# A two-layer graph kernel on one core: the softmax sums of layer 1 made on VectorE with two small matmuls, in place of matmuls with ones over all columns

## The chip, the cores and the metric

The kernel runs on one core of a Trainium2 chip. The metric is the device time of one launch in microseconds, as the median of several runs. The time before is 2396.18 us, the median of 3 runs (2393.23 to 2396.19).

## The reference

64 graphs of 256 nodes with 512 features, and a 0/1 adjacency matrix for each. Two layers, all in float32:

```python
# layer 0 (one head)
fp     = x @ fc_w.T + fc_b                                   # [256, 512]
logits = (fp @ q_w.T + q_b) + (fp @ k_w.T + k_b).T           # [256, 256]
masked = leaky_relu(logits + (1 - adj) * -1e9, 0.01)
x1     = softmax(masked) @ fp + x
# layer 1 (8 heads of 64)
Q, K, V = x1 @ W_q + b_q, x1 @ W_k + b_k, x1 @ W_v + b_v
a, c    = x1 @ w_g[:512], x1 @ w_g[512:]
scores  = Q @ K.T / 8 + a[:, None] + c[None, :] + b_g + log(adj + 1e-9)
out     = softmax(scores) @ V + x1
```

A term that is the same for a whole row of scores falls out of a softmax. So in layer 1 the weight of node i for node j is exp(Q_i K_j / 8 + c_j) * (adj + 1e-9), divided by its sum over j. That sum, one for each of 8 heads and 256 nodes of a graph, is what the change is about.

## The kernel before

Two graphs make a group (`GP = 2`, 512 tokens), and there are 32 groups (`NG`). The products of 512 by 512 are done in a form with seven half-size products (`Product`, whose pieces are `p1` to `p7`, with `keep_*` read out by ScalarE and `sum_*` added by VectorE). Their matmuls all have line L399, their names are `pf` (layer 0's feature product, on the mixed features), `pq`, `pk` and `pv`.

The order of the work is written out by hand: in `step` and `attention_and_layer_0`, strings of piece names are issued one after the other, and each engine runs its instructions in that order. One step holds pieces of four groups: the end of layer 1 of `d` (D), the attention of `a` (A), layer 0 and the projections of `f` (F), and the loads and layer 0's logits of `n` (X). A step with all four begins, in this order, with:

- `pv.sum_11` (VectorE, L427), `scores:0` (TensorE L786, with two exponentials on ScalarE, L800), `sums` (layer 0's sums by products with ones, TensorE L583, read out by ScalarE, L588), `scores:1`, `pv.p3`, `pv.p4`;
- `mix:0` to `mix:3` (TensorE L614, then ScalarE L620), with `ysum` (VectorE L339), `recip` (L592, L593), and D's `divide:1` (VectorE L891), `complete:1` (L899) and `store:1` (DMAs on SP, L929);
- the product `pf`, whose results `pf.sum_*` (VectorE L485) are turned and sent through DRAM and back (`send`, VectorE L717 and SP L721; `fetch`, SP L732) to be there with features on the partitions (`x1T`);
- among these, A's `scores:2`, `attend:0` (TensorE L826, ScalarE L833), `sums_1:0`, `scores:3`, and later `attend:1`, `sums_1:1`;
- then `xsum` (VectorE L364), `pq.*` and `pk.*`, with `keys` (VectorE L500), A's `complete:0 store:0`, A's `turn:1` (VectorE L871) and `ratios_t:1` (L903), the dots of the next group (`dot_q`, `dot_k`, L500), its mask (`adjt`, L536), `residual` (ScalarE L757) and `turn_residual` (VectorE L771), `pv.*` and `weights` (VectorE L570, L574, ScalarE L575).

The attention keeps its weights as e[j, head, i] with j on the partitions, in two halves `jc`. `factor:u:jc` (VectorE L806) multiplies by the adjacency, and `both:u` (L813) adds the two halves, into `esum[u]`: 128 partitions by four heads by 256 nodes, with u = 0, 1 for the first graph and u = 2, 3 for the second. The sum over j is then over the 128 partitions:

- `sums_1:gr` (TensorE L842) does it with eight matmuls whose stationary operand is 32 columns, one of ones and the others zero, and whose moving operand is 256 columns of `esum`; four stand side by side in the array. The result is one bank, copied by ScalarE to `sms1` (L849).
- `ratios_t:gr` (VectorE L903) turns it by blocks of 32 by 32, and `ratios_r:gr` takes the reciprocal (L876) and spreads it over the partitions as `divide` needs it (L879, and four copies of 32 partitions, L882).
- `divide:gr` (L891) multiplies the turned output `osb` by it; `complete:gr` (L899) adds the residual.

PSUM has four single banks that go round (`bank`) and two pairs for the scores (`pair`). `pk.p2` takes the bank that `pq.sum_00` (VectorE L427) has read last. The reciprocals of several groups are kept (`recip1`, `NR` groups) and are compared with a range from time to time (`check`, `in_range`, L938 to L945). The last group has an order of its own at the end of `step` (`n is None`).

Of the kernel before, what the change touches and what calls it, by code (L numbers as in the profile page):

```python
# [25 lines left out]
def kernel(  # L26
# [17 lines left out]
    b_g: bass.AP,  # L44
    out: bass.AP,
):

# [41 lines left out]
    nc = tc.nc  # L89
# [63 lines left out]
    wq_row = const.tile([P, D], F32, tag="wq_row", name="wq_row")  # L153
    kqc = const.tile([P, 1], F32, tag="kqc", name="kqc")

    NR = 8
    recip0 = const.tile([P, NG, T], F32, tag="recip0", name="recip0")
    recip1 = const.tile([P, NR, GP, 2, N // B], F32, tag="recip1", name="recip1")

    def fast():  # L160
        main = ExitStack()
        with main:
# [45 lines left out]
            nc.gpsimd.memset(ones, 0.0)  # L208
            for n in range(2):
                nc.gpsimd.memset(ones[:, n, n : n + 1], 1.0)  # L210

            fc_nat = one.tile([P, T, D], F32, tag="xT", name="fc_nat")
            for c in range(NC):
# [70 lines left out]
            def constants_of_projections():  # L284


                pc = bank("pc")[:, 0:HALF]
                for c in range(NC):
                    for n, (w, o) in enumerate(((wq_sb, 0), (wq_sb, 1), (wv_sb, 0), (wv_sb, 1))):
                        nc.tensor.matmul(  # L290
                            pc[ts(n, RS), :], lhsT=fcb_col[:, c : c + 1].to_broadcast([P, RS]),
                            rhs=w[:, c, o * HALF : (o + 1) * HALF],
                            start=(c == 0), stop=(c == NC - 1), tile_position=(0, n * RS),
                            skip_group_check=True,
                        )
                rows = one.tile([P, HALF], F32, tag="st", name="pc_rows")
                nc.scalar.copy(rows, pc)

                def add():
                    pt = bank("pct")  # L300
                    for m in range(2):
                        nc.tensor.transpose(pt[:, ts(m, P)], rows[:, ts(m, P)], ident)
                    cols = pt[:, 0 : 2 * P].rearrange("p (m n r) -> p n m r", m=2, r=RS)
                    for n, col in enumerate((bq_col, bq_col, bv_col, bv_col)):
                        half = col[:, ts(n % 2, 2)]
                        nc.vector.tensor_tensor(half, half, cols[:, n, :, 0], ALU.add)
                    nc.vector.tensor_tensor(bv_col, bv_col, fcb_col, ALU.add)

                return add
# [195 lines left out]
            class Group:  # L505
# [70 lines left out]

                def sums(self):

                    sm = bank(f"sm0_{self.g}")[:, 0:P]
                    for jc in range(TPG):  # L580
                        for t in range(T):
                            gr, ic = divmod(t, TPG)
                            nc.tensor.matmul(  # L583
                                sm[ts(t, RS), :], lhsT=ones[:, 0, :], rhs=self.e0[:, jc, gr, ts(ic, P)],
                                start=(jc == 0), stop=(jc == TPG - 1), tile_position=(0, t * RS),
                            )
                    self.sms = one.tile([P, P], F32, tag="sms", name=f"sms_{self.g}")
                    nc.scalar.copy(self.sms, sm)  # L588
# [226 lines left out]
                def attend(self, gr):  # L815
# [3 lines left out]
                    for hg in range(2):  # L819
# [12 lines left out]
                                    )  # L832
                        nc.scalar.copy(self.oTs[gr][:, hg, :], po)  # L833

                def sums_1(self, gr):

                    g = self.g

                    sm = bank(f"sm_{g}_{gr}")[:, 0:N]
                    for hg in range(2):  # L840
                        for n in range(4):
                            nc.tensor.matmul(  # L842
                                sm[ts(n, RS), :], lhsT=ones[:, hg, :],
                                rhs=self.esum[2 * gr + hg][:, n // 2, n % 2, :],
                                start=(hg == 0), stop=(hg == 1), tile_position=(0, n * RS),
                                skip_group_check=True,
                            )
                    self.sms1[gr] = one.tile([P, N], F32, tag="sms1", name=f"sms1_{g}_{gr}")
                    nc.scalar.copy(self.sms1[gr], sm)  # L849

                def sums_of_e(self, gr):

                    g = self.g
                    sm = bank(f"sm_{g}_{gr}")[:, 0:N]
                    for hg in range(2):
                        for jc in range(TPG):
                            for n in range(4):
                                nc.tensor.matmul(
                                    sm[ts(n, RS), :], lhsT=ones[:, hg, :],
                                    rhs=self.e[2 * gr + hg, jc][:, n // 2, n % 2, :],  # L860
                                    start=(hg == 0 and jc == 0), stop=(hg == 1 and jc == TPG - 1),
                                    tile_position=(0, n * RS), skip_group_check=True,
                                )
                    self.sms1[gr] = one.tile([P, N], F32, tag="sms1", name=f"sms1_{g}_{gr}")
                    nc.scalar.copy(self.sms1[gr], sm)

                def turn(self, gr):
# [4 lines left out]

                def ratios_r(self, gr):
                    g, nb = self.g, N // B
                    rc = recip1[:, g % NR, gr]
                    nc.vector.reciprocal(rc, self.st.rearrange("p (b c) -> p c b", c=B)[:, 0:2, :])  # L876

                    rs = two.tile([P, 2, 2, nb], F32, tag="rs", name=f"rs_{g}_{gr}")
# [6 lines left out]
                    self.rs = rs  # L885

                def divide(self, gr):

# [1 line left out]
                    blocks = self.osb.rearrange("p (m c) -> p m c", c=B)  # L890
                    nc.vector.tensor_tensor(  # L891
                        blocks, blocks,
                        rs.rearrange("p a n b -> p (a n b)").unsqueeze(2).to_broadcast(
                            [P, NC * nb, B]
                        ), ALU.mult,
                    )
# [2 lines left out]
                    nc.vector.tensor_tensor(self.osb, self.osb, self.xb[gr], ALU.add)  # L899

                def ratios_t(self, gr):
                    self.st = one.tile([P, N], F32, tag="st", name=f"st_{self.g}_{gr}")
                    nc.vector.transpose(self.st, self.sms1[gr])  # L903

                def finish(self, gr):
# [4 lines left out]
                    for hg in range(2):  # L910
# [2 lines left out]
                        nc.vector.transpose(o, self.oTs[gr][:, hg, :])  # L913
                        nc.vector.tensor_tensor(  # L914
                            blocks, blocks,
                            self.rs[:, hg].rearrange("p n b -> p (n b)").unsqueeze(2).to_broadcast(
                                [P, 2 * nb, B]
                            ), ALU.mult,
                        )
# [10 lines left out]

            def in_range(lo, hi, name):

                n0, n1 = (hi - lo) * T, (hi - lo) * T * NH
# [14 lines left out]
            def attention_and_layer_0(D, A, F, X, check):  # L948

                A("pv.sum_11 scores:0")  # L950
                F("sums")
                A("scores:1 pv.p3 pv.p4 factor:0:0 factor:0:1 both:0 factor:1:0 pv.sum_10")
                A("factor:1:1 both:1")
                D("ratios_r:1")
                check()
                F("mix:0 mix:1 ysum:0 recip")
                D("divide:1")
                A("residual:1")
                F("mix:2 mix:3 ysum:1 ysum:2 ysum:3")
                D("complete:1 store:1")  # L960
                F("pf.p1 pf.keep_1 pf.p2 pf.p6 pf.sum_00 begin send:0:0 fetch:0:0")
                A("turn_residual:1")
                F("pf.p7 pf.p5")
                A("scores:2 attend:0 sums_1:0 scores:3 factor:2:0 factor:2:1")
                F("pf.sum_11 send:1:1 fetch:1:1")
                A("both:2 turn:0 ratios_t:0 factor:3:0")
                F("pf.p3 pf.sum_01 send:0:1 fetch:0:1")
                A("factor:3:1 both:3")
                F("pq.p1 pq.keep_1 pf.p4 pf.sum_10 send:1:0 fetch:1:0")
                A("attend:1 sums_1:1 ratios_r:0 divide:0")  # L970
                F("pk.p1 pk.keep_1")

            def check_ranges():
# [9 lines left out]

                return flag_ready

            checked = {}

            def step(d, a, f, n, check):

# [20 lines left out]
                    F("pq.p1 pq.keep_1 pk.p1 pk.keep_1")  # L1010
                F("xsum:0 xsum:1 xsum:2 pq.p6 keys:2 keys:3 keys:0 keys:1")
                X("load_x")
                A("complete:0 store:0")
                F("pq.p7 xsum:3")
                A("turn:1 ratios_t:1")
                F("pq.p2 pq.sum_00 pq.p5 pk.p2 pq.sum_11 copy:0 pq.p3 copy:1 copy:2 pk.sum_00 pq.p4")
                X("dot_q:0")
                F("pq.sum_10")
                X("dot_q:1 dot_q:2 dot_q:3 spread adjt")
                F("pk.p6 pk.p7 pk.p5 residual:0")  # L1020
# [2 lines left out]
                X("dot_k:2 dot_k:3")  # L1023
                F("turn_residual:0 pv.p1 pv.keep_1 pk.p3 pk.p4 pk.sum_10")
                if n is None:
                    A("ratios_r:1 divide:1 complete:1 store:1")
                    F("residual:1 turn_residual:1")

                    F("pv.p2 scores:0 pv.p6 pv.sum_00 factor:0:0 factor:0:1 scores:1 both:0 pv.p7")
# [8 lines left out]
                X("weights:0")  # L1038
                F("pv.sum_00 pv.p7 pv.p5")
                X("weights:1")  # L1040

            with tc.manual_schedule(engines=ENGINES):
                f = Group(0)
# [234 lines left out]
```

## Time and profile before

| | |
|---|---|
| median of 3 runs | 2396.18 us |
| the profiled execution | 2395.4 us, its span 2393.6 us |
| granted clock of TensorE | 0.998 |
| PE, busy | 2376.3 us, 99% |
| DVE (VectorE), busy | 1841.4 us, 77% |
| ACT (ScalarE), busy | 1002.9 us, 42% |
| `sums_1`: L842 on PE, 1008 records | 67.5 us |
| `ratios_t`: L903 on DVE, 64 | 25.8 us |
| `ratios_r`: L876, L879, L882 on DVE | 14.7, 11.6, 42.6 us |
| one step in the middle (1181.45 to 1254.90) | 73.45 us; PE busy 73.45, DVE 57.02, ACT 31.13 |

PE is TensorE's matmuls, PEld its weight loads. A float32 matmul of the program has two records in the profile, each with a weight load of its own. Where matmuls lie side by side in the array, the busy time counts their union once. A line of the timeline gives start, duration, engine, source line, operation, the tile written and the tiles read, the shape and the number of instructions merged; a number in brackets at its end is idle time before it, with what ended it.

### The profile page before, as it was taken

The page shows a single profiled execution, that of the slowest core. Times are in us where ns is not written, and L with a number is a line of the kernel's source. Part 1 is how long each engine was busy: PE and PEld are TensorE (multiplying, and loading weights), DVE is VectorE, ACT ScalarE, POOL GpSimd, SP SyncE. Part 2 cuts the span into 40 slices and gives each one's busy share as a digit, 9 for nine tenths or more (in the row PEclk, how much of TensorE's full clock was granted, in tenths as well). Part 3 has the DMA queues.
Part 4 walks back from the last instruction along what each step waited for, and adds up shares of the span by engine and source line. Part 5 has one row for each costly group of instructions (what it writes and reads, how often), then busy time and mean ns, then how long its engine had stood idle before and what let it go on. Part 6 is the DMA issues. An engine that isn't in the chain of part 4 may idle for free.

```text
span 2393.6 us, 36233 instructions
## 1 busy us (share of the span) xinstructions
PE 2376.3 (99%) x13947; PEld 1917.8 (80%) x13947; DVE 1841.4 (77%) x3126; ACT 1002.9 (42%) x1772; POOL 143.5 (6%) x103
## 2 busy tenths in 40 slices
PE   9999999999999999999999999999999999999997
PEld 5888787888878888888887888787888877887886
DVE  6778777777777778777878777777778877787776
ACT  3444344444344343444434443444444444443443
POOL 0000000000000000000000000000000000000000
PEclk9999999999999999999999999999999999999999
DMA  4122322323322333223232232332233322223212
GB/s 128 45 62 67 84 71 58 62 62 84 78 65 57 62 76 84 71 54 62 67 84 71 58 64 61 84 81 68 52 66 71 84 71 54 62 66 85 71 49 37
DMA packets 517274, 164.00 MB, mean 69 GB/s; under 512 B 415188, under 2 KB 478696, under 8 KB 517096
## 3 DMA queue, kind: packets, MB, share of 16 engines
q1 hardware_dynamic: 514440, 160.32, 29.6%
q8 instruction: 112, 1.84, 0.3%
q10 hardware_dynamic: 2656, 1.31, 0.2%
q14 instruction: 66, 0.54, 0.1%
HBM read 95.43 MB, written 66.12 MB: 67 GB/s over the span
## 4 chain that ended last, share of the span: by engine, by line
PE 98%; DVE 1%; DMA 1%; issue 0%; ACT 0%; SPq 0%; ACTq 0%; DVEq 0%
PE pv L399 16%; PE pk L399 16%; PE pq L399 16%; PE pf L399 16%; PE sc L786 10%; PE oT L826 9%; PE y L614 9%; PE sm L842 3%; PE sm L583 1%; PE fp L643 1%; DMA fc_nat<-in_L_gnn_fc_w_dram 0%; DMA x1T<-xd 0%; DMA xd<-xt 0%; PE rc L592 0%; DVE osb L914 0%
## 5 line engine op out<-in xcount | busy, mean ns | idle before, releaser
L806 DVE TENSOR_TENSOR e<-e,am 128x1024 f32<-128x1024 f32 x254 | 303.4, 1216 | 129.5 <-ACT e L800 129.5
L800 ACT ACTIVATE e<-sc,c 128x1024 f32<-128x1024 f32 x254 | 269.2, 1111 | 37.8 <-PE sc L786 37.7
L479 POOL TENSOR_TENSOR pf_s<-pf_s,x 128x512 f32<-128x512 f32 x93 | 142.6, 1533 | 2167.7 <-ACT pf_s L478 2099.1
L786 PE MATMUL sc<-qT,kT 64*128 64x256 f32 x2048 | 255.8, 389 | 0.0
L786 PEld LDWEIGHTS sc<-qT,kT 64*128 64x128 f32 x2048 | 184.9, 186 | 60.5 <-issue 34.3
L826 PE MATMUL oT<-e,v 128*64 128x256 f32 x2032 | 233.4, 382 | 0.0
L614 PE MATMUL y<-e,x 128*128 128x256 f32 x992 | 222.6, 379 | 0.0
L826 PEld LDWEIGHTS oT<-e,v 128*64 128x64 f32 x2032 | 140.2, 137 | 85.5 <-issue 21.3
L614 PEld LDWEIGHTS y<-e,x 128*128 128x128 f32 x992 | 186.1, 190 | 26.3
L416 ACT ACTIVATE pq_s<-pq,cols 128x256 f32<-128x256 f32 x192 | 80.5, 470 | 251.3 <-PE pq L399 251.3
L478 ACT ACTIVATE pf_s<-pf,recip 128x256 f32<-128x256 f32 x186 | 78.0, 470 | 199.4 <-PE pf L399 199.4
L813 DVE TENSOR_TENSOR es<-e,e 128x1024 f32<-128x1024 f32 x126 | 154.4, 1225 | 3.8
L427 DVE TENSOR_TENSOR qT<-pq,pq_s 128x512 f32<-128x512 f32 x96 | 65.1, 678 | 113.3 <-PE pq L399 72.4
L427 DVE TENSOR_TENSOR v<-pv,pv_s 128x512 f32<-128x512 f32 x96 | 66.1, 689 | 111.8 <-ACT pv_s L413 77.5
L833 ACT COPY oTs<-oT 128x512 f32<-128x512 f32 x128 | 75.0, 586 | 182.9 <-PE oT L826 161.9
L413 ACT COPY pk_s<-pk 128x512 f32<-128x512 f32 x96 | 56.2, 585 | 192.4 <-PE pk L399 141.5
L620 ACT COPY yT<-y 128x512 f32<-128x512 f32 x124 | 72.0, 580 | 152.5 <-PE y L614 152.5
L413 ACT COPY pv_s<-pv 128x512 f32<-128x512 f32 x96 | 55.6, 579 | 185.8 <-PE pv L399 185.8
L399 PE MATMUL pk<-x1T,wk 128*128 128x256 f32 x512 | 125.1, 387 | 0.2
L399 PE MATMUL pq<-x1T,wq 128*128 128x256 f32 x512 | 121.1, 379 | 0.2 <-issue 0.2
L399 PE MATMUL pv<-wv,t1b 128*128 128x256 f32 x512 | 121.1, 379 | 0.0
L399 PE MATMUL pv<-wv,t1b_c 128*128 128x256 f32 x512 | 121.0, 379 | 0.0
(164 smaller groups left out, 4453.6 us busy)
## 6 DMA issues: line engine op xcount, KB each, us to landing
x<-in_x_dram SPq DMA_DIRECT2D x32, 1024.0 KB, 5.5
out_dram<-osb SPq DMA_DIRECT2D x254, 128.0 KB, 3.9
xd<-xt SPq DMA_DIRECT2D x124, 256.0 KB, 2.1
x1T<-xd SPq DMA_DIRECT2D x496, 64.0 KB, 2.0
adj<-in_adj_dram SPq DMA_DIRECT2D x128, 128.0 KB, 5.1
qrow<-q SPq DMA_DIRECT2D x31, 256.0 KB, 4.5
fc_nat<-in_L_gnn_fc_w_dram ACTq DMA_DIRECT2D x4, 256.0 KB, 4.3
wq<-in_L_gnn_W_q_dram SPq DMA_DIRECT2D x1, 1024.0 KB
```

Of the source, the lines that this page charges most:

```text
L399: nc.tensor.matmul(o, lhsT=lk[:, ts(m, P)] if len(lk.shape) == 2 else lk[:, m], rhs=rk, start=(start and m == 0 and k == 0), stop=(m == 1 ...
L413: nc.scalar.copy(dst, src)
L416: nc.scalar.activation(dst[:, m], src[:, m], AF.Identity, bias=self.bias[:, 2 * o + m : 2 * o + m + 1],)
L427: nc.vector.tensor_tensor(self.out(o, k), src, s, ALU.add)
L478: nc.scalar.mul(s[:, m], src[:, m], self.recip[:, TPG * k + m : TPG * k + m + 1])
L479: nc.gpsimd.tensor_tensor(s, s, self.out(o, k), ALU.add)
L614: nc.tensor.matmul(y[:, ts(gr, N)], lhsT=self.x[:, gr * TPG + j, ts(c, P)], rhs=self.e0[:, j, gr, :], start=(gr == 0 and j == 0), stop=(gr ...
L786: nc.tensor.matmul(sc[:, par, pr, :], lhsT=self.kT[rows, 2 * hg + pr, ts(t, P)], rhs=self.qT[rows, 2 * hg + pr, ts(gr, N)], start=True, st ...
L800: nc.scalar.activation(e, sc, AF.Exp, bias=self.c[:, t : t + 1], scale=SCALE)
L806: nc.vector.tensor_tensor(ef, ef, self.am[:, jc, u // 2, :].unsqueeze(1).to_broadcast([P, 4, N]), ALU.mult,)
L813: nc.vector.tensor_tensor(self.esum[u], self.e[u, 0], self.e[u, 1], ALU.add)
L826: nc.tensor.matmul(oT[par * HD : (par + 1) * HD, pr, :], lhsT=self.v[:, gr * TPG + jc, ts(h, HD)], rhs=self.e[2 * gr + hg, jc][:, par, pr, :],
```

## The change

The sum over the 128 partitions is made in two parts, without `sums_1` (which stays for the last group alone). `parts:u`, on VectorE, turns `esum[u]` (128 by 1024) by blocks of 32 by 32 and adds up each run of 32 elements, which leaves 128 by 32. `totals`, on TensorE, then adds the four blocks of 32 partitions: two matmuls for a graph, each with a stationary operand `every` of 128 by 64 (a column of identity blocks) and 32 moving columns, one for each half of the output partitions. The result already stands as `divide` needs it, and `ratios:gr` is one reciprocal from PSUM.

`totals_1` (for D's second graph) writes into spare columns of the bank in which `sums` makes layer 0's sums; `totals_0` (for A's first graph) has a bank of its own. The turned tiles take buffers of other tiles (`osb`, `e0`, `adj`) at times when these are free. In the order, `parts:0` comes after `divide:1`, `parts:1` after `turn_residual:1`, `parts:2` after `dot_q:0`, and `parts:3` after `weights:1`, at the end of the step; `both:2`, `both:3` and `divide:0` are moved later; `sums_1`, `ratios_t` and `ratios_r` go. The range is compared for four groups at a time (`NR = 4`). The diff, cut to its core:

```diff
-    NR = 8
+    NR = 4
...
-    recip1 = const.tile([P, NR, GP, 2, N // B], F32, tag="recip1", name="recip1")
+    recip1 = const.tile([P, NR, GP, NC, N // B], F32, tag="recip1", name="recip1")
...
+            every = const.tile([P, HD], F32, tag="every", name="every")
+            for q in range(P // B):
+                for n in range(HD // B):
+                    rows = slice(q * B, (q + 1) * B)
+                    nc.gpsimd.tensor_copy(every[rows, ts(n, B)], ident[rows, rows])
...
                 def sums(self):
-                    sm = bank(f"sm0_{self.g}")[:, 0:P]
+                    sm0["bank"] = bank(f"sm0_{self.g}")
+                    sm = sm0["bank"][:, 0:P]
...
+                def parts(self, u):
+                    g, (gr, hg), nb = self.g, divmod(u, 2), NC * N // B
+                    if hg == 0:
+                        self.part = two.tile([P, 2, nb], F32, tag="part", name=f"part_{g}_{gr}")
+                    pool, tag = ((two, "osb"), (one, "e0"), (one, "e0"), (one, "adj"))[u]
+                    turned = pool.tile([P, NC * N], F32, tag=tag, name=f"est_{g}_{u}")
+                    nc.vector.transpose(turned, self.esum[u].rearrange("p a b i -> p (a b i)"))
+                    nc.vector.tensor_reduce(
+                        self.part[:, hg, :], turned.rearrange("p (m c) -> p m c", c=B),
+                        AX.X, ALU.add,
+                    )
+
+                def totals(self, gr, dst):
+                    half = NC * N // B // 2
+                    for par in range(2):
+                        nc.tensor.matmul(
+                            dst[par * HD : (par + 1) * HD, :].rearrange("p (a m) -> p a m", a=2),
+                            lhsT=every, rhs=self.part[:, :, par * half : (par + 1) * half],
+                            start=True, stop=True, skip_group_check=True,
+                        )
+                    self.tot = dst
+
+                def totals_1(self):
+                    self.totals(1, sm0["bank"][:, P : P + NC * N // B])
+
+                def totals_0(self):
+                    self.totals(0, bank(f"tot_{self.g}_0")[:, 0 : NC * N // B])
+
+                def ratios(self, gr):
+                    self.rs = recip1[:, self.g % NR, gr]
+                    nc.vector.reciprocal(self.rs.rearrange("p m b -> p (m b)"), self.tot)
...
             def attention_and_layer_0(D, A, F, X, check):
                 A("pv.sum_11 scores:0")
                 F("sums")
-                A("scores:1 pv.p3 pv.p4 factor:0:0 factor:0:1 both:0 factor:1:0 pv.sum_10")
-                A("factor:1:1 both:1")
-                D("ratios_r:1")
+                D("totals_1")
+                A("scores:1 pv.p3 pv.p4 factor:0:0 factor:0:1")
+                D("ratios:1")
+                A("both:0 factor:1:0 pv.sum_10 factor:1:1 both:1")
                 check()
                 F("mix:0 mix:1 ysum:0 recip")
                 D("divide:1")
-                A("residual:1")
+                A("parts:0 residual:1")
                 F("mix:2 mix:3 ysum:1 ysum:2 ysum:3")
                 D("complete:1 store:1")
                 F("pf.p1 pf.keep_1 pf.p2 pf.p6 pf.sum_00 begin send:0:0 fetch:0:0")
-                A("turn_residual:1")
+                A("turn_residual:1 parts:1")
                 F("pf.p7 pf.p5")
-                A("scores:2 attend:0 sums_1:0 scores:3 factor:2:0 factor:2:1")
+                A("scores:2 attend:0 totals_0 scores:3 factor:2:0 factor:2:1")
                 F("pf.sum_11 send:1:1 fetch:1:1")
-                A("both:2 turn:0 ratios_t:0 factor:3:0")
+                A("ratios:0 turn:0 factor:3:0")
                 F("pf.p3 pf.sum_01 send:0:1 fetch:0:1")
-                A("factor:3:1 both:3")
+                A("factor:3:1")
                 F("pq.p1 pq.keep_1 pf.p4 pf.sum_10 send:1:0 fetch:1:0")
-                A("attend:1 sums_1:1 ratios_r:0 divide:0")
+                A("attend:1 both:2 both:3")
                 F("pk.p1 pk.keep_1")
...
-                A("complete:0 store:0")
+                A("divide:0 complete:0 store:0")
                 F("pq.p7 xsum:3")
-                A("turn:1 ratios_t:1")
+                A("turn:1")
                 F("pq.p2 pq.sum_00 pq.p5 pk.p2 pq.sum_11 copy:0 pq.p3 copy:1 copy:2 pk.sum_00 pq.p4")
                 X("dot_q:0")
+                A("parts:2")
                 F("pq.sum_10")
...
                 if n is None:
-                    A("ratios_r:1 divide:1 complete:1 store:1")
+                    A("parts:3")
+                    if a is not None:
+                        a.totals(1, bank("tot_last")[:, 0 : NC * N // B])
+                    A("ratios:1 divide:1 complete:1 store:1")
...
                 X("weights:1")
+                A("parts:3")
```

More of the change, by code (lines that the diff above doesn't have):

```diff
@@ L295, in constants_of_projections @@
                         )
-                rows = one.tile([P, HALF], F32, tag="st", name="pc_rows")
+                rows = two.tile([P, HALF], F32, tag="xt", name="pc_rows")
                 nc.scalar.copy(rows, pc)
@@ L847, in sums_1 @@
                             )
-                    self.sms1[gr] = one.tile([P, N], F32, tag="sms1", name=f"sms1_{g}_{gr}")
+                    self.sms1[gr] = two.tile([P, N], F32, tag="xt", name=f"sms1_{g}_{gr}")
                     nc.scalar.copy(self.sms1[gr], sm)
@@ L863, in sums_of_e @@
                                 )
-                    self.sms1[gr] = one.tile([P, N], F32, tag="sms1", name=f"sms1_{g}_{gr}")
+                    self.sms1[gr] = two.tile([P, N], F32, tag="xt", name=f"sms1_{g}_{gr}")
                     nc.scalar.copy(self.sms1[gr], sm)
@@ L874, in ratios_r @@
                     g, nb = self.g, N // B
-                    rc = recip1[:, g % NR, gr]
+                    rc = two.tile([P, 2, nb], F32, tag="rc", name=f"rc_{g}_{gr}")
                     nc.vector.reciprocal(rc, self.st.rearrange("p (b c) -> p c b", c=B)[:, 0:2, :])
-                    rs = two.tile([P, 2, 2, nb], F32, tag="rs", name=f"rs_{g}_{gr}")
+                    rs = recip1[:, g % NR, gr].rearrange("p (h n) b -> p h n b", h=2)
                     nc.vector.tensor_copy(rs, rc.unsqueeze(2).to_broadcast([P, 2, 2, nb]))
@@ L884, in ratios_r @@
                         )
-                    self.rs = rs
+                    self.rs = recip1[:, g % NR, gr]
                 def divide(self, gr):
@@ L892, in divide @@
                         blocks, blocks,
-                        rs.rearrange("p a n b -> p (a n b)").unsqueeze(2).to_broadcast(
+                        rs.rearrange("p m b -> p (m b)").unsqueeze(2).to_broadcast(
                             [P, NC * nb, B]
@@ L901, in ratios_t @@
                 def ratios_t(self, gr):
-                    self.st = one.tile([P, N], F32, tag="st", name=f"st_{self.g}_{gr}")
+                    self.st = one.tile([P, N], F32, tag="sms1", name=f"st_{self.g}_{gr}")
                     nc.vector.transpose(self.st, self.sms1[gr])
@@ L915, in finish @@
                             blocks, blocks,
-                            self.rs[:, hg].rearrange("p n b -> p (n b)").unsqueeze(2).to_broadcast(
+                            self.rs[:, ts(hg, 2)].rearrange("p n b -> p (n b)").unsqueeze(2).to_broadcast(
                                 [P, 2 * nb, B]
@@ L931, in in_range @@
             def in_range(lo, hi, name):
-                n0, n1 = (hi - lo) * T, (hi - lo) * T * NH
+                n0, n1 = (hi - lo) * T, (hi - lo) * GP * NC * N // B
                 ok = one.tile([P, n0 + n1], F32, tag="junk", name=f"ok_{name}")
@@ L984, in check_ranges @@
                 return flag_ready
-            checked = {}
+            checked, sm0 = {}, {}
             def step(d, a, f, n, check):
```

## The prediction

> **What bounds the kernel now.** First the page, part 1 and the chain that ended last, for the engine that sets the end:
>
> ```profile
> PE 2376.3 (99%) x13947; PEld 1917.8 (80%) x13947; DVE 1841.4 (77%) x3126; ACT 1002.9 (42%) x1772; POOL 143.5 (6%) x103
> ...
> PE 98%; DVE 1%; DMA 1%; issue 0%; ACT 0%; SPq 0%; ACTq 0%; DVEq 0%
> ```
>
> TensorE is the chain, so a microsecond off it counts, and so does any wait put on it. Then the waits of the weight loads (total, times, longest):
>
> ```profile
> PEld pk L399 <- DVE qT L427: 3.6, 9, 0.4
> ...
> PEld pq L399 <- DVE t1b L364: 2.7, 6, 1.1
> ```
>
> Small, but they name the one place where VectorE is already as late as it may be: `pk.p2`, which writes the bank that `pq.sum_00` (L427) must first have read. Third, one step in order of time (start, duration), 1181.45 to 1254.90 = 73.45 us, in which PE is busy for 73.45. PE:
>
> ```profile
> 1183.38 0.65 PE L583 MATMUL sm<-e,ones 128*32 128x128 f32 x16
> 1183.95 2.00 PE L786 MATMUL sc<-qT,kT 64*128 64x256 f32 x16
> ...
> 1192.89 0.27 PE L592 MATMUL rc<-ident,sms 128*128 128x128 f32 x1
> 1193.00 3.62 PE L614 MATMUL y<-e,x 128*128 128x256 f32 x16
> ...
> 1210.71 1.07 PE L842 MATMUL sm<-es,ones 128*32 128x256 f32 x16
> 1211.71 2.00 PE L786 MATMUL sc<-qT,kT 64*128 64x256 f32 x16
> ...
> 1217.20 1.89 PE L399 MATMUL pf<-fcT,tb 128*128 128x256 f32 x8
> ...
> 1222.62 1.07 PE L842 MATMUL sm<-es,ones 128*32 128x256 f32 x16
> 1223.62 1.99 PE L399 MATMUL pk<-x1T,wk 128*128 128x256 f32 x8
> ```
>
> ScalarE beside the first two lines, and the weight load of `pk.p2`:
>
> ```profile
> 1182.63 2.12 ACT L800 ACTIVATE e<-sc,c 128x1024 f32<-128x1024 f32 x2
> 1184.64 0.27 ACT L588 COPY sms<-sm 128x128 f32<-128x128 f32 x1
> ```
>
> ```profile
> 1232.14 0.62 PEld L399 LDWEIGHTS pk<-x1T,wk 128*128 128x128 f32 x3
> ```
>
> VectorE on the way there:
>
> ```profile
> 1218.44 1.23 DVE L813 TENSOR_TENSOR es<-e,e 128x1024 f32<-128x1024 f32 x1
> 1219.58 0.87 DVE L485 SCALAR_TENSOR_TENSOR x<-pf,recip,pf_s 128x256 f32<-128x256 f32 x2
> ...
> 1231.10 0.40 DVE L903 STREAM_TRANSPOSE st<-sms 128x256 f32<-128x256 f32 x1
> 1231.42 0.65 DVE L427 TENSOR_TENSOR qT<-pq,pq_s 128x512 f32<-128x512 f32 x1
> ```
>
> `pq.sum_00` ends at 1232.07 and the load that needs it starts at 1232.14: 0.07 us, and the nine waits show 0.05 to 0.06 us from VectorE's end to a held load. There is no slack.
>
> **The terms, us per step.** A step's frame is the old times above; an offset moves all that follows.
>
> *Matmuls removed.* L842 fills 1210.71 to 1211.71 and 1222.62 to 1223.62: 1.00 each, twice a step, 31 steps (the last group keeps its own).
>
> *The two matmuls added.* Each has two records; two column halves stand side by side, so two rounds of 32 columns. Nearest rows: the single L592 takes a slot of 0.11 (1192.89 to 1193.00); L583, sixteen records four abreast, takes 0.57 (1183.38 to 1183.95), 0.14 a round. So 0.11 to 0.57; I take 0.2 in the flow (two rounds shorter than L583's) and 0.37 after a wait, when the first load (137 ns for 128x64, L826) is no longer hidden. `totals_0` follows `attend:0` in the flow; its sums (`parts:1`) are made in VectorE's idle 3.29 us before L806 at 1207.51. Net 0.2 - 1.00 = -0.80, x31 = **-24.8**.
>
> *`totals_1` gets a new wait.* It writes columns of the same bank as `sums`. In the changed order it waits for VectorE's `parts:3` and for ScalarE's copy of that bank (L588). `parts:3` is early (weights end near 1179.7, plus 2.4). The copy is not: it stands behind two exponentials and ends at 1184.91, while PE is at 1183.95. Behind the waiting matmul stand `scores:1`, `pv.p3`, the whole step. Price: 0.96 + 0.06 + 0.37 = 1.39, x30 = **+41.7**. ScalarE's two copies less (L849, 0.37) come later in the step and do not help.
>
> *The second sum removed, and VectorE late.* Without L842 at 1222.62, `pk.p2`'s load would stand at 1232.14 - 1.00 = 1231.14 against `pf.p4`. VectorE's way from `pf.p4` to `pq.sum_00`: was 1219.58 to 1232.07, 12.49. It starts 0.45 earlier (`pf.p4` ends 1219.09, and `both:3` no longer stands ahead). Gone: the ratios of L876 to L882 (1.20 before `divide:0`) and L903 (0.32). New on it: `both:2` and `both:3`, 2 x 1.145 by the steps of L813. `divide:0` only moves inside it, but now directly precedes `complete:0`, which needs it: +0.12 (a dependent L813 follows after 1.25, an independent one after 1.14). 12.49 - 1.52 + 2.29 + 0.12 = 13.38, end 1232.51, load 1232.57: a wait of 1.42. So 1.42 - 1.00 = +0.42, x31 = **+13.0**. The saving is more than eaten by the queue in front of L427.
>
> *Landings.* With the queue begun earlier, `xsum:0` can start at 1222.96, not 1223.46. In nine or ten steps its DMA lands later than that; they lose up to 0.5 more than now: **+4.6** (0 to 8).
>
> *VectorE's new work.* Four times a step a turn (128x1024, 1.24) and a reduce. The reduce rows are 128x144 at 303 ns and 128x288 at 453, 1.04 ns an element: 1024 give 1.22 (below, L806's 1.22; above, twice that). 124 x 2.46 = +305 us, less 62 x 1.47 for what goes, plus 62 x 0.25 for reciprocals: DVE 1841 to about 2070, 85% of the new span. Covers: `parts:3` the 2.48 us wait for `pv_s` before 1182.23; `parts:0` idle 1.51 before 1197.27, and `ysum:1` then ends near 1200.0, before `pf.p6` (1199.9 + 1.39); `parts:1` as said; `parts:2` idle 2.16 before 1237.74 and 1.02 before 1248.10. All hold at 1.22: 0 on the path. At twice the cost `parts:0` and `parts:2` lose cover, together about 1.0 a step, +31.
>
> The Trainium skill's "VectorE: DVE Perf Modes" (Rules for kernel authors) speaks against this part: a `tensor_reduce` on the hot path runs at one element a cycle and should be restructured. By its 0.96 GHz an estimate is 1.07 us plus a fixed cost; the rows say 1.22 and, at that, off the path, so the sum is the same by both.
>
> *Last step.* `parts:3` and the totals stand on VectorE and PE between `pk.sum_10` and `pv.p2`: L427 ends at 2352.93, `parts:3` near 2355.3, PE would go on at 2351.8: **+3.7**. The eight copies that make `every` on GpSimd: 0, its next work is in the second step (bound 1). Four more range checks of 1.7: VectorE's margin before `pf.p6` then is 0.4, so 0. `load_adj` now waits for `parts:3` on SP, with `store:1` behind it; that store comes 18 us later: 0. The store of `divide:0` moves 0.5 on SP: 0.
>
> *New holes in PE.* The clock granted now is 1.00 over the step, with no hole to show what a hole does. "TensorE: Matmul & The Clock Gate" of the skill (Why this matters for your kernels) asks for no idle over about 3 us, or the clock halves; the two holes here are 1.0 and 1.4, so the sum keeps full clock; only the last step's hole reaches that, about 2 us by an estimate from the page. No run here shows it.
>
> **Sum.** -24.8 + 41.7 + 13.0 + 4.6 + 3.7 = +38.2. The profiled execution took 2395.4 (span 2393.6): 2433.6. It lies 0.8 under the median, 2396.18: **2434**.
>
> **Rivals.**
> 1. *Only the bank wait is real* (faster). If VectorE reached L427 by 1231.08, 1.4 us earlier than I count, the second sum is a clean -1.00 x31: -24.8 - 31.0 + 41.7 + 3.7 = -10.4, **2386**. For it: VectorE is idle 16 us in a step. Against: not one of those idle stretches lies between `pf.p4` and L427. Chance 0.04. With the bank wait gone too (`totals_1` at 0.2): 2350, chance 0.02; the wait stands in the order.
> 2. *Only VectorE's wait is real*: `totals_1` passes at 0.2: +2.5, **2399**, chance 0.03.
> 3. *The reduce costs twice the row's slope*: **2465**, chance 0.10.
> Forecast 0.81.
>
> **Range and chances.** 0.15 on each of 61 pairs is 9, landings 4, VectorE's wait by 0.1 is 3: 2420 to 2448 for the forecast; rival 3's half-way pulls the top: 2418 to 2460. What a measurement of this kernel tells from no change is 0.2%, 4.8 us. Faster 0.06 (rival 1), same 0.03 (rival 2), slower 0.91.
>
> **What would show it.** Right: steps near 74.5; an idle of about 1.0 before `totals_1`, ended by ACT L598's copy of sms, and of 1.4 before `pk.p2`, ended by DVE qT; PE busy down by some 45 and a few per cent idle; DVE near 85%. Wrong: steps under 73.4, no idle before the first totals, or a reduce of 128x1024 far from 1.22 us.

## The result and the profile after

The changed kernel takes 2421.42 us (median of 4 runs, 2419.18 to 2421.78) against 2394.76 (4 runs of the kernel before beside it, 2393.23 to 2396.19). The ratio is 1.0109, with a 95% interval from 1.0092 to 1.0127: slower, by some 27 us. The profiled execution took 2419.18, its span 2417.4, which is 23.8 more than before. The sum of the prediction said +38.2.

The page of the changed kernel, part 1 and the chain that ended last:

```profile
PE 2335.3 (97%) x13203; PEld 1908.1 (79%) x13203; DVE 2093.0 (87%) x3026; ACT 979.6 (41%) x1710; POOL 130.3 (5%) x111
...
PE 71%; DVE 14%; DMA 5%; ACT 4%; issue 3%; SPq 2%; DVEq 0%; ACTq 0%
```

TensorE works 41 us less and the kernel takes 24 more. Of the chain, TensorE had 98% and now has 71%; VectorE, DMA and ScalarE have come into it. The waits of TensorE say where (engine, tile, line, what it waited for; total us, times, longest):

```profile
PE sm L863 <- ACT sms L598: 28.3, 30, 1.2
PE pk L408 <- DVE qT L436: 28.2, 31, 0.9
PE pq L408 <- DVE t1b L373: 6.6, 11, 1.0
PE pok L1024 <- DVE okp_last L991: 5.0, 1, 5.0
PE tot_last L863 <- DVE part L853: 3.3, 1, 3.3
```

The first two are new; they come in every step that has the instruction (30 and 31). `sm L863` is the pair of small matmuls of `totals_1`, held by ScalarE's copy L598 (L588 before). `pk L408` is `pk.p2`, held by VectorE's `pq.sum_00`. The wait for `t1b` (`xsum:1`, which follows `xsum:0` and its landing) had 0.7 us in all before. `tot_last` is the last step's; `pok` stood there before as well.

One step in the timeline, the lines that answer to those of before. TensorE:

```profile
1190.54 0.64 PE L593 MATMUL sm<-e,ones 128*32 128x128 f32 x16
1192.12 0.31 PE L863 MATMUL sm<-part,every 128*64 128x32 f32 x4 [0.94 <-ACT sms L598]
1192.36 2.00 PE L796 MATMUL sc<-qT,kT 64*128 64x256 f32 x16
...
1215.52 3.67 PE L836 MATMUL oT<-e,v 128*64 128x256 f32 x32
1219.02 0.26 PE L863 MATMUL tot<-part,every 128*64 128x32 f32 x4
1219.21 2.00 PE L796 MATMUL sc<-qT,kT 64*128 64x256 f32 x16
...
1226.51 3.67 PE L836 MATMUL oT<-e,v 128*64 128x256 f32 x32
1230.12 1.99 PE L408 MATMUL pk<-x1T,wk 128*128 128x256 f32 x8
...
1240.02 1.99 PE L408 MATMUL pk<-x1T,wk 128*128 128x256 f32 x8 [0.91 <-DVE qT L436]
1241.85 1.89 PE L408 MATMUL pq<-x1T,q_s 128*128 128x256 f32 x8
```

ScalarE before the wait of `totals_1`:

```profile
1189.80 2.12 ACT L810 ACTIVATE e<-sc,c 128x1024 f32<-128x1024 f32 x2
1191.80 0.27 ACT L598 COPY sms<-sm 128x128 f32<-128x128 f32 x1
```

VectorE before the wait of `pk.p2`:

```profile
1226.62 0.88 DVE L494 SCALAR_TENSOR_TENSOR x<-pf,recip,pf_s 128x256 f32<-128x256 f32 x2 [0.72 <-PE pf L408]
...
1228.17 2.32 DVE L823 TENSOR_TENSOR es<-e,e 128x1024 f32<-128x1024 f32 x2
1230.40 0.69 DVE L373 TENSOR_TENSOR t1b<-x1T 128x512 f32<-128x512 f32 x1
...
1235.15 1.22 DVE L937 TENSOR_TENSOR osb<-osb,recip 128x1024 f32<-128x1024 f32 x1
1236.40 1.23 DVE L945 TENSOR_TENSOR osb<-osb,xb 128x1024 f32<-128x1024 f32 x1
...
1239.31 1.40 DVE L436 TENSOR_TENSOR qT<-pq,pq_s 128x512 f32<-128x512 f32 x2
```

`both:2` and `both:3` (2.32 together) and `divide:0` (1.22) stand between `pf.sum_10` and `pq.sum_00`, with no idle time of VectorE between them. The last line is two instructions; the first, 0.65 long in the step of before, then ends at 1239.96, and `pk.p2` starts at 1240.02.

The 31 steps, cut at starts of TensorE's matmuls, show what the step lost and won. Each row is the sum over all steps of the time from the first named start to the second:

| stretch of the step | before | after | difference | predicted |
|---|---|---|---|---|
| `scores:0` to `scores:1` (`sums`, `totals_1`) | 77.7 | 115.1 | +37.5 | +41.7 |
| `scores:2` to `scores:3` (`attend:0`, `sums_1:0` or `totals_0`) | 202.5 | 174.2 | -28.3 | -24.8 |
| `scores:3` to `pk.p1` (`attend:1`, `sums_1:1`) | 369.2 | 338.2 | -31.0 | -31.0 |
| `pk.p1` to `pq.p6` (waits for landings) | 58.1 | 66.3 | +8.2 | +4.6 |
| `pq.p6` to `pk.p2` to `pq.p3` | 271.3 | 306.4 | +35.1 | +44.0 |
| last step from `pq.p3` on | 33.8 | 37.6 | +3.8 | +3.7 |
| up to the first full step | 76.8 | 75.0 | -1.8 | 0 |

The rest of the step is unchanged to 0.001 us, in every step but one (0.145 shorter): 21.230 from `scores:1` to `scores:2`, 20.813 from `pq.p3` to the next `scores:0`. VectorE's `parts` did not lengthen either stretch. The rows add to 23.5; of the 0.3 that is missing, 0.4 lies behind the last row and -0.1 in that one step.

### The profile page after: what moved, and what is told of

The parts are those of the page before. It is cut to its first block, busy times and chain, and to the rows that moved or that the text cites. A ratio compares the mean times of both kernels' runs of the same rounds, so it can differ in the third digit from the quotient of the medians.

```text
span 2417.4 us, 34590 instructions
## 1 busy us (share of the span) xinstructions
PE 2335.3 (97%) x13203; PEld 1908.1 (79%) x13203; DVE 2093.0 (87%) x3026; ACT 979.6 (41%) x1710; POOL 130.3 (5%) x111
## 4 chain that ended last, share of the span: by engine, by line
PE 71%; DVE 14%; DMA 5%; ACT 4%; issue 3%; SPq 2%; DVEq 0%; ACTq 0%
PE pv L408 16%; PE pk L408 14%; PE pf L408 14%; PE y L624 9%; PE sc L796 7%; PE pq L408 5%; PE oT L836 4%; DVE t1b L373 3%; DVE jc L509 3%; ACT e L810 3%; DMA xd<-xt 3%; DMA x1T<-xd 2%; SPq L742 2%; DVE osb L917 2%; DVE osb L937 1%
## 5 line engine op out<-in xcount | busy, mean ns | idle before, releaser
L488 POOL TENSOR_TENSOR pf_s<-pf_s,x 128x512 f32<-128x512 f32 x93 | 128.1, 1377 | 2200.8 <-ACT pf_s L487 2090.6
L853 DVE TENSOR_REDUCE part<-est 128x32 f32<-128x1024 f32 x124 | 151.3, 1220 | 4.2
L408 PE MATMUL pk<-x1T,wk 128*128 128x256 f32 x512 | 127.4, 392 | 28.2 <-DVE qT L436 28.2
L852 DVE STREAM_TRANSPOSE est<-es 128x1024 f32<-128x1024 f32 x124 | 152.4, 1229 | 0.0
L823 DVE TENSOR_TENSOR es<-e,e 128x1024 f32<-128x1024 f32 x126 | 148.4, 1197 | 1.2
L408 PEld LDWEIGHTS pk<-x1T,wk 128*128 128x128 f32 x512 | 92.3, 190 | 62.5 <-DVE qT L436 40.6
L436 DVE TENSOR_TENSOR kT<-pk,pk_s 128x512 f32<-128x512 f32 x96 | 66.3, 690 | 74.9 <-PE pk L408 69.8
```

Source lines behind the costliest of these rows:

```text
L408: nc.tensor.matmul(o, lhsT=lk[:, ts(m, P)] if len(lk.shape) == 2 else lk[:, m], rhs=rk, start=(start and m == 0 and k == 0), stop=(m == 1 ...
L436: nc.vector.tensor_tensor(self.out(o, k), src, s, ALU.add)
L488: nc.gpsimd.tensor_tensor(s, s, self.out(o, k), ALU.add)
L823: nc.vector.tensor_tensor(self.esum[u], self.e[u, 0], self.e[u, 1], ALU.add)
L852: nc.vector.transpose(turned, self.esum[u].rearrange("p a b i -> p (a b i)"))
L853: nc.vector.tensor_reduce(self.part[:, hg, :], turned.rearrange("p (m c) -> p m c", c=B), AX.X, ALU.add,)
```

## The experiments

Theory: two queue placements cost the time, and nothing else does. `totals_1` waits for a bank that ScalarE reads late, with the whole step behind it, and VectorE has too much queued between `pf.p4` and `pq.sum_00`. The rival: VectorE's new work itself, 250 us more, is what makes the kernel slower.

**`totals_1` issued behind `scores:1`**, so that TensorE has 2 us of other work while ScalarE copies.

```diff
-                D("totals_1")
-                A("scores:1 pv.p3 pv.p4 factor:0:0 factor:0:1")
+                A("scores:1")
+                D("totals_1")
+                A("pv.p3 pv.p4 factor:0:0 factor:0:1")
```

> The changed kernel, with totals_1 issued after scores:1 and not before it; VectorE's order and work are untouched. Theory (two queues decide: ScalarE's copy in front of totals_1, VectorE's queue in front of pk.p2): the copy is done by then, the piece from scores:0 to pv.p3 loses about 1.0 us a step, 30 steps, so 2421 - 30 = about 2391. Rival A (VectorE's load of 87% slows the kernel wherever the work stands): no change, 2421. Rival B (the short matmuls and the changes of tile shape cost, not the wait): no change or slower, 2421 to 2425.

Measured 2391.86 (10 runs; ratio to before 0.9991, 0.9982 to 1.0001), 30 less than the changed kernel. In its timeline of TensorE the pair follows without a wait:

```profile
1177.38 0.65 PE L593 MATMUL sm<-e,ones 128*32 128x128 f32 x16
1177.96 2.00 PE L796 MATMUL sc<-qT,kT 64*128 64x256 f32 x16
1179.89 0.31 PE L863 MATMUL sm<-part,every 128*64 128x32 f32 x4
1180.12 1.99 PE L408 MATMUL pv<-v_s,t1b_c 128*128 128x256 f32 x8
```

`scores:0` to `scores:1` is back at 77.7, and the pair takes 0.24 where it now stands (1179.89 to 1180.12). The wait of `pk.p2` is as before (28.1 us, 31 times), so the two waits do not depend on each other.

**`totals_1` in its place, with a bank of its own.**

```diff
-                    self.totals(1, sm0["bank"][:, P : P + NC * N // B])
+                    self.totals(1, bank(f"tot_{self.g}_1")[:, 0 : NC * N // B])
```

> The changed kernel, with totals_1 at its place but in a bank of its own and not in spare columns of the bank of sums. Theory: the wait came from the shared bank alone, so from scores:0 to scores:1 3.75 goes to about 2.75, 2421 - 30 = 2391, as e1. If it came from parts:3 or from the change of tile shape, no change, 2421; if the four banks get short by it, a new wait before the mix, up to 2405.

Measured 2394.27 (10 runs; 0.9994, 0.9984 to 1.0003), 27 less than the changed kernel. The pair stands directly behind `sums`, without idle time:

```profile
1178.62 0.65 PE L593 MATMUL sm<-e,ones 128*32 128x128 f32 x16
1179.19 0.31 PE L863 MATMUL tot<-part,every 128*64 128x32 f32 x4
1179.43 2.00 PE L796 MATMUL sc<-qT,kT 64*128 64x256 f32 x16
```

So `parts:3` was never late here, and the wait came from the shared bank alone. Whether the chip needs this wait or only the program's bookkeeping of the bank asks for it, no run tells apart. The pair costs 0.24 in this place too.

**VectorE's queue before `pk.p2` mended**: `divide:0` back ahead of `xsum:0`, `both:2` behind `pq.sum_11`, `both:3` behind `turn_residual:0`.

```diff
-                A("attend:1 both:2 both:3")
+                A("attend:1 divide:0")
...
-                A("divide:0 complete:0 store:0")
+                A("complete:0 store:0")
...
-                F("... pk.p2 pq.sum_11 copy:0 pq.p3 copy:1 copy:2 pk.sum_00 pq.p4")
+                F("... pk.p2 pq.sum_11")
+                A("both:2")
+                F("copy:0 pq.p3 copy:1 copy:2 pk.sum_00 pq.p4")
...
-                F("turn_residual:0 pv.p1 pv.keep_1 pk.p3 pk.p4 pk.sum_10")
+                F("turn_residual:0")
+                A("both:3")
+                F("pv.p1 pv.keep_1 pk.p3 pk.p4 pk.sum_10")
```

> The changed kernel, with divide:0 back before xsum:0, both:2 behind pq.sum_11 and both:3 behind turn_residual:0; the same instructions on every engine, only VectorE's order differs. Theory: the queue from pf.p4 to pq.sum_00 is short again (xsum:0 at its DMA's landing, some 3.6 us after pf.p4, then 8.3 to the end of pq.sum_00), so pk.p2 waits for nothing: from pq.p6 to pk.p2 8.05 goes to 6.91, about -1.15 - 0.1 a step, 31 steps, 2421 - 38 = 2383; steps with a late landing give back a few. Rival A: no change, 2421. Rival B: no change, 2421.

Measured 2385.81 (6 runs; 0.9966, 0.9954 to 0.9979), 36 less than the changed kernel. `pq.p6` to `pk.p2` went from 249.7 to 215.6, below the 216.8 of before. What TensorE waits for in this kernel:

```profile
PE sm L863 <- ACT sms L598: 28.3, 30, 1.2
PE pq L408 <- DVE t1b L373: 7.5, 12, 1.4
```

The wait of `pk.p2` is gone and that of `totals_1` untouched. VectorE in one step:

```profile
1213.96 1.18 DVE L937 TENSOR_TENSOR osb<-osb,recip 128x1024 f32<-128x1024 f32 x1
1216.05 0.69 DVE L373 TENSOR_TENSOR t1b<-x1T 128x512 f32<-128x512 f32 x1 [0.90 <-DMA x1T<-xd]
...
1223.70 0.65 DVE L436 TENSOR_TENSOR qT<-pq,pq_s 128x512 f32<-128x512 f32 x1
```

VectorE stands idle for 0.90 until the DMA lands, and is still in time. From `xsum:0` to the end of `pq.sum_00` it now needs 8.30, in the changed kernel 9.56.

**`both:3` alone moved**, to see whether less than the whole move is enough.

```diff
-                A("attend:1 both:2 both:3")
+                A("attend:1 both:2")
...
-                F("turn_residual:0 pv.p1 pv.keep_1 pk.p3 pk.p4 pk.sum_10")
+                F("turn_residual:0")
+                A("both:3")
+                F("pv.p1 pv.keep_1 pk.p3 pk.p4 pk.sum_10")
```

> The changed kernel, with both:3 alone taken off the way (behind turn_residual:0); both:2 stays in front of xsum:0 and divide:0 behind keys. Theory 1 (only the length of VectorE's queue from pf.p4 counts): 1.15 less a step, as much as pk.p2's wait, 2421 - 35 = 2386, as e2. Theory 2 (the way has a second part: xsum:0 cannot start before its DMA lands, some 3.6 us after pf.p4, so what stands in front of xsum:0 is filler and only what stands behind it counts): xsum:0 starts 0.2 to 0.3 earlier in the steps with an early landing and no earlier in the others, 2421 - 5 = 2413 to 2418.

Measured 2424.21 (4 runs; 1.0118, 1.0101 to 1.0135): no gain, and both expectations missed. The waits of TensorE and of VectorE in this kernel:

```profile
PE sm L863 <- ACT sms L598: 28.4, 30, 1.2
PE pk L408 <- DVE qT L436: 27.7, 31, 0.9
```

```profile
DVE t1b L373 <- DMA x1T<-xd: 42.7, 31, 2.3
```

VectorE reaches `xsum:0` a full `both` earlier and then waits for the DMA, in 31 steps instead of 11 (7.3 us in the changed kernel). `xsum:0` reads what `send:0:1`, the last but one, has sent. From the end of that `send` to the start of `xsum:0` the median is 5.73 us, in the changed kernel 5.66. So the changed kernel's VectorE was already about as late as the landing, and what stands behind `xsum:0` starts at nearly the same time with `both:3` ahead of it or without. What shortened the way in the run before was the move of `divide:0`: ahead of `xsum:0` it fills the wait for the landing, behind it it delays `pk.p2` (8.30 against 9.56 above). The moves of `both:2` and `both:3` made room for it there; no run moves `divide:0` alone. My estimate of the landing, 3.6 us after `pf.p4`, holds for the earliest alone: here `xsum:0` starts 3.64 to 5.09 us after the end of `pf.p4`, 3.94 in the median. The profile of before could not show this, since VectorE's own queue (6.17 from the same `send`) hid the landing in most steps.

**Both queues mended**, the edits of the first and of the third run together.

> Both edits, e1 and e2, together. Theory: the two waits are in series and independent, so they add: 2421 - 30 - 38 = about 2353, and a step falls to some 71.8 us; VectorE then has 29% less idle time than TensorE's step leaves now and may show a wait of its own, so up to 2365. Rival A: 2421 or a little less, above the kernel before. Rival B: 2421.

Measured **2355.30** (4 runs, 2354.92 to 2356.59; 0.9841, 0.9825 to 0.9857): the change is a gain of 38 us over the kernel before, and 66 under the kernel as changed. The gains in the ratio nearly add up: 0.0118 and 0.0143 for the two edits by themselves, 0.0268 for both.

```profile
PE 2327.1 (99%) x13203; PEld 1908.0 (81%) x13203; DVE 2081.5 (88%) x3026; ACT 980.9 (42%) x1710; POOL 130.5 (6%) x111
```

VectorE executes the same 3026 instructions as in the changed kernel (busy for 2081.5 us, there 2093.0) and is at 88%; TensorE is at 99% again. A step without a late landing is 71.78 us, of 73.45 before.

A second execution of this kernel, profiled for its landings, took 2358.89, above the 2353 to 2357 expected of it. `pq.p6` waited 8.0 us for `t1b` in 11 steps, in the first trace 7.3 in 10. In both traces the eight waits above 0.5 us fall on the same steps, the first and every fourth after it; why, no run shows.

**The kernel before with one instruction of 1.22 us more on VectorE**, a maximum of `xb` with itself (128x1024), which changes no value; no part of the change is in it. First behind `divide:0`, on the way to `pk.p2`:

```diff
+                def again(self, gr):
+                    nc.vector.tensor_tensor(self.xb[gr], self.xb[gr], self.xb[gr], ALU.max)
...
-                A("attend:1 sums_1:1 ratios_r:0 divide:0")
+                A("attend:1 sums_1:1 ratios_r:0 divide:0 again:0")
```

> The kernel before, with one more VectorE instruction a step, a 128x1024 maximum of xb with itself (1.22 us, no value changes), behind divide:0, that is on the way from pf.p4 to pq.sum_00. TensorE's work is that of before. Theory: there is no slack on that way, so nearly the whole of it shows at pk.p2: 1.15 + 0.1 a step, less in the nine steps with a late landing: 2395 + 30 to 38 = 2425 to 2433. Rival A (VectorE's load, 77% to 79%): nothing or a few us, 2395 to 2400.

Then the same instruction behind `turn_residual:1`, where VectorE was idle for 3.29:

```diff
-                A("turn_residual:1")
+                A("turn_residual:1 again:1")
```

> The kernel before with the same extra VectorE instruction as in e4 (128x1024 maximum of xb with itself), behind turn_residual:1, where VectorE waits 3.29 us for an exponential. Theory: the place decides, so nothing: 2393 to 2396. Rival A (VectorE's load): the same as e4, 2422.

Measured 2421.99 (4 runs; 1.0121, 1.0104 to 1.0138) on the way, and 2394.54 (10 runs; 0.9997, 0.9987 to 1.0006) beside it. One instruction a step, 38 us of work in all, costs 27 to 29 us or nothing. The first page reads:

```profile
PE 2388.7 (99%) x13947; PEld 1914.2 (79%) x13947; DVE 1875.7 (78%) x3157; ACT 1002.8 (41%) x1772; POOL 143.3 (6%) x103
```

VectorE is at 78% and the kernel as slow as the changed one at 87%: the rival, VectorE's load, is refuted from both sides. The time on the way came a little under what was expected. An undisturbed step grew by 1.015, less than the instruction's slot of 1.14, and the steps with late landings no longer cost extra, since the longer queue covers them. The delay also shows at another place than was expected. `pk.p2` is not the first to be late; `pq.p6` is, which needs `xsum:1` from the same queue:

```profile
PE pq L399 <- DVE t1b L364: 13.8, 31, 0.5
```

`pq.p6` starts 0.61 later in each step, and from there to `pq.p3`, past `pk.p2`, another 0.40 are lost. The page counts these 0.40 as busy time: 12.4 us more than before for the same matmuls.

**The last step's wait as well**: on top of both queues, `tot_last` issued behind `pv.p2` and the last group's first scores, so that the 3.3 us for `parts:3` pass beside work.

```diff
+                    F("pv.p2 scores:0")
...
-                    F("pv.p2 scores:0 pv.p6 pv.sum_00 factor:0:0 factor:0:1 scores:1 both:0 pv.p7")
+                    F("pv.p6 pv.sum_00 factor:0:0 factor:0:1 scores:1 both:0 pv.p7")
```

> The kernel with both queues mended (totals_1 behind scores:1; divide:0, both:2 and both:3 placed by their due times), 2355.3 us, and with one more move: in the last step tot_last, which there makes TensorE wait 3.3 us for VectorE's parts, comes behind pv.p2 and the last group's first scores, whose operands are ready. My theory (the wait is only a matter of what stands behind it in TensorE's queue): the 3.3 us wait of tot_last goes, total 2352.0, between 2351 and 2353. Rival: VectorE, which makes these parts and the last group's other sums, is what the last step waits for anyway (the last step took 33.8 us before the change and 40.3 us with both queues mended), so that the wait only moves to a later matmul: 2355, unchanged.

Measured 2354.27 (4 runs, 2353.49 to 2355.60; 0.9830, 0.9814 to 0.9846): 1.0 lower, not to be told apart from 2355.30, and above the 2351 to 2353 of the theory. In the trace both were partly right. The last step fell from 40.26 to 35.97, but a part of the wait came back one sum later, at the last group's `sums_1` (1.8 us, `PE sm L888` for VectorE's `es`), and in this execution the start took 1.1 and the late landings 2.2 more than in the other.

That 40.26 holds something else. The wait for `tot_last` is 3.28 us in every kernel that has it, but what follows differs. The changed kernel:

```profile
2375.05 0.31 PE L863 MATMUL tot_last<-part,every 128*64 128x32 f32 x4 [3.28 <-DVE part L853]
2375.28 1.99 PE L408 MATMUL pv<-wv,t1b_c 128*128 128x256 f32 x8
2377.21 2.00 PE L796 MATMUL sc<-qT,kT 64*128 64x256 f32 x16
```

The kernel with both queues mended, and its windows of 2 us (the seventh column of figures, behind POOL, is the granted clock):

```profile
2309.91 0.43 PE L863 MATMUL tot_last<-part,every 128*64 128x32 f32 x4 [3.28 <-DVE part L853]
2310.27 3.78 PE L408 MATMUL pv<-wv,t1b_c 128*128 128x256 f32 x8
2313.98 2.79 PE L796 MATMUL sc<-qT,kT 64*128 64x256 f32 x16
```

```profile
2306.00:2308.00 2.00, 0.63 (x3) 0.20 (x2) 1.39 (x3) 1.12 (x3) 0.00 (x0) 1.00 0.00 0
2308.00:2310.00 2.00, 0.09 (x2) 0.12 (x4) 1.73 (x2) 0.00 (x0) 0.00 (x0) 0.70 0.00 0
2310.00:2312.00 2.00, 2.00 (x8) 1.67 (x9) 1.58 (x2) 0.00 (x0) 0.00 (x0) 0.50 0.00 0
2312.00:2314.00 2.00, 2.00 (x7) 1.08 (x6) 1.87 (x2) 0.00 (x0) 0.00 (x0) 0.50 0.00 0
2314.00:2316.00 2.00, 2.00 (x13) 1.69 (x14) 1.17 (x2) 0.04 (x1) 0.00 (x0) 0.59 0.66 102
2316.00:2318.00 2.00, 2.00 (x14) 1.51 (x11) 0.90 (x1) 2.00 (x2) 0.00 (x0) 1.00 0.96 144
```

During the hole the clock falls to 0.50 and stays there until about 2315.6; the next two pieces take 6.57 instead of 3.99, so the hole of 3.28 costs 2.6 more. In the traces of six kernels and of a second execution of the one above (2358.89) there are seven such holes, all of 3.28. In six the clock was halved, for 3.4 us in two and for 6.8 in four, and their last steps are 1.6 to 2.9 us longer than the changed kernel's, which lost none. The kernel with `both:3` alone has the longest (2.95). The changed kernel's three other executions took 2421.36 to 2421.78, its profiled one 2419.18; whether their clock was halved there no trace shows.

## Why the prediction was right, and where its sizes were off

The call (slower, 0.91) and the range (2418 to 2460) held; the time, 2434, was 12.6 too high. The mechanism is the predicted one: two places on TensorE, released by the named instructions, 0.94 and 0.91 idle a step (about 1.0 and 1.4 were predicted). Rivals 1 and 2 each took one of the two places as harmless. Run alone, each mended place gave 30 and 36 us, so neither was. Rival 3 is gone by one row: the reduce takes 1220 ns, the turn 1229.

```profile
L853 DVE TENSOR_REDUCE part<-est 128x32 f32<-128x1024 f32 x124 | 151.3, 1220 | 4.2
```

By terms:

- *Matmuls removed*: right, 1.00 each (-31.0 for `sums_1:1`).
- *The two matmuls added*: mis-sized. In the flow behind `attend:0` the pair costs 0.09, not 0.2 (the stretch fell by 0.913), 3.5 us in all. After the wait it costs 0.24, not 0.37: 4.2 us with the 0.01 by which the wait was off. The mistake was to hold the row of L592 (0.11 for one record of 128 columns) as a lower end and lean to L583, whose sixteen records are of another shape. `attend`'s are 128*64 like the pair's. The pair's own slot there is 0.19 (1219.02 to 1219.21), as predicted, but `attend:0` ahead of it takes 3.50 where it took 3.60 ahead of `sums_1:0`.
- *The wait of `totals_1`*: right. By the pace of `sums` (0.57) the pair could start at 1191.11 and starts at 1192.12, 1.01 later, for 0.96 plus 0.06, and it waits for the copy named. The 0.94 of the profile counts from the end of `sums` by its record (0.64).
- *VectorE late at `pk.p2`*: the queue was counted right. From the start of `pf.sum_10` to that of `pq.sum_00` it is 12.69, by the prediction's sum 12.73. The price was not: 35.1 over `pq.p6` to `pq.p3` where 44.0 was counted. I moved `pk.p2` by as much as its weight load. Before, the load stood 0.22 ahead of its matmul, hidden behind others; after the wait matmul and load start together (1240.01 and 1240.02), and only half of that gap is lost again in the next 1.8 us. So a held load costs TensorE some 0.1 us less than it is late. And 3.7 of the 271.3 before were waits that late steps had at this place already (31 times the undisturbed 8.634 is 267.6); they do not come on top of the new one.
- *Landings*: +8.2 against +4.6, just outside its bounds (0 to 8). The run with `both:3` alone showed why: VectorE had come down to the usual time of the landing, 5.7 us after the end of `send:0:1`, so that every later landing counts in full.
- *VectorE's work*: 2093.0, predicted about 2070. The reciprocals from PSUM take 319 to 352 ns where 250 was counted. More comes from `complete`: 22 of its 66 instructions take 2.29 us where none took longer than 1.22 before, 23.8 in all, and each of the 22 started while GpSimd was at work on `pf_s`. None of this reached TensorE, and the covers held, as the two unchanged stretches show.
- *Last step*: +3.8 for +3.7. The halved clock that I reckoned with there as possible, outside the sum, did not come in this execution, and did in all six others that have the same hole. That the row fits so well is in part luck.
- *Start*: -1.8, not in the sum, and luck. TensorE's wait there for the first load of `fc_nat` was 1.6 before and 0.6 after, and the matmuls ahead of it took 3.45 and 2.74. The first full step starts between 75.0 and 78.4 in the kernels run, and between 75.3 and 76.8 in the three of them that have no part of the change.

The rule of the Trainium skill that I had set against `parts` ("VectorE: DVE Perf Modes", Rules for kernel authors: restructure a `tensor_reduce` on the hot path) was the wrong place to look, since this reduce is not on the path that sets the end, but for the 3.28 us of the last step; the two fastest kernels here have VectorE at 88%.

On the holes, the Trainium skill's "TensorE: Matmul & The Clock Gate" (The HAM clock gate) has a window of about 3.4 us that runs freely, so that its phase decides. The runs agree in kind: 61 holes of 0.9 to 1.2 us left the mean clock at 0.998, and one of 3.28, a little shorter than that window, halved it in six executions and not in the seventh. Where the window stood in each, no run shows.

## What to carry to other kernels

Where one engine is busy for 99% of the span, look at each instruction that the change puts into its queue and ask who must be done before it, and at each instruction put into another engine's queue ahead of something the first one waits for; the totals of busy time say nothing of this, as one instruction of 1.22 us a step cost 27 to 29 us or none by its place alone. A matmul that borrowed spare columns of a bank waited here for that bank's reader, so put it behind other work or give it its own bank. Where a queue waits for a landing, fill it ahead of the landing and not behind; work that is pulled out ahead of it gains nothing once the landing is what comes last.

## What the runs showed that was not expected

- Two matmuls of 32 columns (four records) behind matmuls of the same 128*64 shape lengthen the stretch by 0.09 us; between other shapes, or after a wait, by 0.24.
- A hole of 3.28 us on TensorE costs another 1.6 to 2.9 us by the clock at 0.50, in six of seven executions; holes of about 1 us, two in each step, cost nothing beyond themselves.
- A landing that is hidden in most steps before (VectorE idle for it 0.15 us a step on the mean) was only half a microsecond from the surface: 1.3 to 1.4 us a step in the kernels that come to it earlier.
- A `complete` (128x1024, 1.22 us on VectorE) that started while GpSimd was at work on `pf_s` took 2.29 us, in 22 of 23 cases.
- `tensor_reduce` of 128x1024 in runs of 32 takes 1220 ns, as long as a product of two tiles of that size (1.22 us).
